# A four-stage kernel on one core: routing ranks made batch by batch, and the tail of the scan moved

## The chip, the cores and the metric

The kernel runs on one core of a Trainium2 chip. The metric is the device time of one execution in microseconds (us). A core has TensorE (PE, with its weight loads PEld), VectorE (DVE), ScalarE (ACT), GpSimd (POOL) and SyncE (SP), which issues most transfers.

## The reference, cut to what matters

Layer 0 is a state-space block over 4 images of 32 x 32 places and 256 channels: a layer norm, a projection to 512, a 3 x 3 depthwise convolution, GELU, a selective scan with 64 states, a second layer norm, a projection back and a residual. Layer 1 is an attention without softmax, then 16 experts of which each token takes two:

```python
xs = ...                                  # scan of 1024 places, 512 channels, 64 states
x = src + (_layernorm(ys + x * D_skip, ln2_g, ln2_b) @ w_out + b_out)
t = to_tokens(x)
qkv = _ln_t(t) @ W_qkv + b_qkv            # q, k: centred by rows
kv = einsum('bnc,bnd->bcd', k2, v)        # k2, q2: squares, normalised
t = t + (v + einsum('bnc,bcd->bnd', q2, kv) / sqrt(N)) @ W_out + b_out
probs = softmax(_ln_t(t) @ gate_w + gate_b); top 2 of 16, weights renormalised
t = t + sum over the two: weight * ((silu(x @ w1) * (x @ w2)) @ w3)
```

## The kernel before, in words

There are 4096 tokens, in 4 batches of 8 tiles of 128 tokens. All work is in fp32 but for a few routing masks in bf16.

**The scan (to about 2802 us).** It goes over 8 units, each half a batch (512 places). In a unit, 64 states times 4 channel blocks make 256 slots. In each slot ScalarE makes a scaled input `bx` (L687) and a decay `da` (L695), PE turns `bx` (L701), VectorE runs the scan `h` (L712); every fourth slot GpSimd multiplies `h` by C (L719), and PE adds the result to a sum `y` in PSUM (L733). This part's order is written out by hand: `beside(u)` hands out lists of pieces of other work (the next units' convolution, `conv`; their step sizes, `dt_bc`; the last unit's layer norm and output, `after`), and each piece goes into a slot where its engine has room. All pieces share one PSUM bank, `bg`. At a unit's end `close_sum` copies `y` to `ysb` (L750).

**The tail (about 2802 to 2842 us).** Nothing stands beside the last half's output: `run(after_stats(u))`, the roots and `run(*after(u, None))` come one after another (L604 to L627), and write to the tensor `td` in memory. Then the weights of attention are loaded (`wqkv`, `wout` and their biases), centred and multiplied together (L949 to L1004: `wcat`, `wvT`, `bvo`, `bcat`), and `t_all` is loaded from `td` (L941).

**Attention (about 2842 to 3088 us).** Outside the hand-written parts a scheduler orders the instructions of each engine by its own costs. A batch makes statistics (L1011), `xh`, its transpose, then for each of 8 tiles `pqk` (L1037), `qk` (L1042), its square `sq` (L1045), `sums` (L1046), `pv` (L1054); then `q2T`, `k2`, `ksq`, `pkv` (L1089), `po` (L1134), the normed tokens `xe`, stored in `xd` (L1150), and the gate: `pgT`, `pg`, and two masks `hots` of each token's experts (L1193). PSUM holds three buffers for `pqk` and `pv` and two for the tag `po`. Much of a batch's gate work stands among the next batch's projections.

**The ordering (about 3088 to 3140 us).** Over all 32 tiles at once: the masks are added (`hot2`, L1220), counted over partitions by two products (`ptot`, `prank`), summed along tiles (`run`, L1230), turned into each expert's number of 128-row blocks and first block (`over`, `nb`, `end`, `first`), each block's expert (`done`, `ef`, `eid`), each pair's slot (`pick`, `sf`), and from it the one-hot masks `qh` (place in block, L1287) and `ih` (block, L1291). Products `pgp` (L1302) of these give each block's rows, `src` and `dst`.

**The experts (about 3140 to 3570 us).** A hand-written order goes over 74 blocks. SyncE reads `eid`, fetches three weights of 512 KB (L1340, L1353; six buffers, four blocks ahead); GpSimd gathers the rows `xb` (L1346) and scatters the result `yb` (L1397). The weights' pool `wp` is opened after the ordering's pools are closed, and the blocks of memory of closed pools are given out again.

**The end (to about 3603 us)** loads both results of each token and adds them (L1439).

## Time and profile before

| | us |
|---|---|
| median of 3 runs | 3609.48 |
| lowest, highest | 3608.98, 3614.11 |
| profiled execution, its time | 3609.15 |
| profiled execution, span from first to last instruction | 3607.3 |

| engine | busy us | share of the span |
|---|---|---|
| PE | 3245.6 | 90% |
| PEld | 2626.9 | 73% |
| DVE | 2981.9 | 83% |
| ACT | 2863.8 | 79% |
| POOL | 2484.2 | 69% |

The shares are means over stages with different limits, so they are read stage by stage: busy time in chosen windows says which engine fills a stage, the chain of waits says what follows on what where no engine does, and the lists by line give the length of one instruction of each kind. Line numbers are those of the kernel before.

### The profile page before, as it was taken

How to read it: one execution, taken by the hardware profiler on the slowest of the kernel's cores; microseconds unless marked ns; L12 is line 12 of the kernel's file. 1: busy time of each engine (PE TensorE's matmuls, PEld its weight loads, DVE VectorE, ACT ScalarE, POOL GpSimd, SP SyncE). 2: the span in 40 equal slices, each digit the busy share in tenths (PEclk: the TensorE clock that was granted, in tenths of full speed). 3: DMA queues.
4: the chain of work that ended last, by engine and by line, in shares of the span. 5: the costliest groups of instructions: out<-in, count | busy, mean ns of one | idle time of the engine just before them, and what ended most of it. 6: DMA issues, size and time to landing. Idle time of an engine off the chain costs nothing.

```text
span 3607.3 us, 60573 instructions
## 1 busy us (share of the span) xinstructions
PE 3245.6 (90%) x22292; PEld 2626.9 (73%) x22292; DVE 2981.9 (83%) x3398; ACT 2863.8 (79%) x4748; POOL 2484.2 (69%) x906
## 2 busy tenths in 40 slices
PE   8989999999998998999999989898999788599995
PEld 3678777777777777777777777777777455399985
DVE  5799999999999999999999999999999666622224
ACT  1799999999999999999999999999999244121211
POOL 0489878987897798879878987998888110033331
PEclk9999999999999999999999999999999999699997
DMA  3223222212222122222222122222121200299996
GB/s 101 64 55 76 56 64 65 61 57 58 71 69 60 62 62 61 64 63 66 60 64 64 57 59 54 55 58 57 55 60 55 73 24 12 100 381 325 319 302 236
DMA packets 355165, 334.41 MB, mean 93 GB/s; under 512 B 162081, under 2 KB 241441, under 8 KB 354866
## 3 DMA queue, kind: packets, MB, share of 16 engines
q1 hardware_dynamic: 334834, 306.21, 29.1%
q0 software_dynamic: 7104, 19.41, 1.6%
q10 hardware_dynamic: 12928, 4.89, 0.5%
q8 instruction: 177, 2.90, 0.3%
q14 instruction: 122, 1.00, 0.1%
HBM read 304.21 MB, written 25.69 MB: 91 GB/s over the span
## 4 chain that ended last, share of the span: by engine, by line
ACT 60%; PE 20%; DMA 8%; DVE 7%; issue 2%; POOL 0%; POOLq 0%; DVEq 0%; ACTq 0%; SPq 0%
ACT da L695 28%; ACT bx L687 28%; DMA yd<-yb,dst 6%; PE ps L701 4%; PE y L733 3%; PE p L1377 3%; DVE h L712 3%; PE pqk L1037 2%; PE bg L382 1%; PE pf L1389 1%; DMA xb<-xd,src 1%; PE pv L1054 1%; PE ps L382 1%; PE ps_t L120 1%; ACT L695 1%
## 5 line engine op out<-in xcount | busy, mean ns | idle before, releaser
L719 POOL TENSOR_TENSOR h<-h,cb_n 128x2048 f32<-128x2048 f32 x512 | 2143.6, 4192 | 416.7 <-DVE h L712 328.0
L701 PE MATMUL ps<-ident,bx 128*128 128x128 f32 x8192 | 1323.3, 283 | 197.8 <-DVE h L712 138.0
L687 ACT ACTIVATE bx<-dtxT,bT 128x512 f32<-128x512 f32 x2048 | 1451.5, 709 | 16.5 <-DVE dtxT L534 16.5
L695 ACT ACTIVATE da<-dt,l_conv_a_log_sb 128x512 f32<-128x512 f32 x2048 | 1452.2, 709 | 13.6 <-DVE h L712 13.3
L701 PEld LDWEIGHTS ps<-ident,bx 128*128 128x128 f32 x8192 | 937.2, 142 | 632.8 <-DVE h L712 307.9
L712 DVE TENSOR_TENSOR_SCAN h<-da,last,ps 128x512 f32<-128x512 f32 x1024 | 1231.6, 1263 | 30.3 <-ACT da L695 21.6
L733 PE MATMUL y<-ident,h 128*128 128x128 f32 x8192 | 1246.1, 275 | 5.7 <-POOL h L719 5.6
L712 DVE TENSOR_TENSOR_SCAN h<-da,ps 128x512 f32<-128x512 f32 x1024 | 1189.5, 1207 | 49.4 <-ACT da L695 32.6
L733 PEld LDWEIGHTS y<-ident,h 128*128 128x128 f32 x8192 | 974.5, 143 | 7.8 <-POOL h L719 6.7
L1383 DVE TENSOR_TENSOR hT<-s,p 128x256 f32<-128x256 f32 x148 | 62.4, 421 | 336.4 <-ACT s L1382 336.4
L1377 PE MATMUL p<-xT,w 128*128 128x128 f32 x2368 | 291.6, 277 | 0.5 <-ACT xT L1366 0.5
L1377 PEld LDWEIGHTS p<-xT,w 128*128 128x128 f32 x2368 | 285.1, 194 | 4.8 <-ACT xT L1366 0.9
L1382 ACT ACTIVATE s<-p 128x256 f32<-128x256 f32 x148 | 56.9, 384 | 275.5 <-PE p L1377 275.5
L1397 POOL DMA_INDIRECT yd<-yb,dst x74 | 73.2, 990 | 264.5 <-DMA yd<-yb,dst 185.9
L382 PE MATMUL bg<-pad,dgc 128*128 128x512 f32 x432 | 222.2, 596 | 0.0
L1346 POOL DMA_INDIRECT xb<-xd,src x74 | 72.1, 975 | 132.8 <-DVE dst L1318 108.7
L1389 PE MATMUL pf<-w,hT 128*128 128x256 f32 x592 | 153.3, 382 | 0.1
L1051 POOL TENSOR_TENSOR t_all<-t_all,bcat 128x256 f32<-128x256 f32 x32 | 23.0, 747 | 164.6 <-ACT xh L1023 159.9
L1389 PEld LDWEIGHTS pf<-w,hT 128*128 128x128 f32 x592 | 101.7, 192 | 8.2 <-DVE hT L1383 0.5
L1366 ACT COPY xT<-px 128x256 f32<-128x256 f32 x74 | 27.6, 372 | 77.5 <-PE px L1364 77.5
L382 PEld LDWEIGHTS bg<-pad,dgc 128*128 128x128 f32 x432 | 65.5, 192 | 0.0
L382 PE MATMUL ps<-pad,dgc 128*128 128x512 f32 x144 | 64.0, 605 | 0.7 <-DVE e L487 0.7
(287 smaller groups left out, 2056.5 us busy)
## 6 DMA issues: line engine op xcount, KB each, us to landing
cb_n<-cd SPq DMA_DIRECT2D x512, 256.0 KB, 3.3
w<-in_L_ffn_w_dram SPq DMA_DIRECT2D x222, 512.0 KB, 6.2
dgc<-diags SPq DMA_DIRECT2D x84, 192.0 KB, 3.1
y<-yd SPq DMA_DIRECT2D x8, 1024.0 KB, 9.6
last<-h SPq DMA_DIRECT2D x256, 2.0 KB, 2.9
xr<-in_x_dram SPq DMA_DIRECT2D x32, 128.0 KB, 3.2
td<-xr SPq DMA_DIRECT2D x32, 128.0 KB, 3.3
t_all<-td SPq DMA_DIRECT2D x4, 1024.0 KB, 10.0
```

The lines of the kernel that those rows point to most:

```text
L382: nc.tensor.matmul(made["bg"].rearrange("p (h w) -> p h w", w=WW), made["dgc", m * 3 + i][:, j, :], pads[m][:, half * ROWS + i : (half + 1 ...
L687: nc.scalar.activation(t, made["dtxT", u][:, j, :], AF.Copy, scale=made["bT", u][:, j, n : n + 1])
L695: nc.scalar.activation(t, made["dt", u][:, m, :], AF.Exp, scale=A[:, m, n : n + 1])
L701: nc.tensor.transpose(t[:, blk(j, P)], made["bx", s, j][:, blk(m, P)], ident)
L712: nc.vector.tensor_tensor_scan(h[:, m, 1:], made.pop(("da", s, m)), made.pop(("dbx", s, m)), 0.0 if seg == 0 else last[b][:, n, m : m + 1] ...
L719: nc.gpsimd.tensor_tensor(h[:, :, :BANK], h[:, :, 1:], over_middle(made["c", s], DK), ALU.mult)
L733: nc.tensor.matmul(made["y", u][j][:, blk(m, P)], made["h", s][:, m, blk(j, P)], ident, is_transpose=True, start=n == 0 and m == 0, stop=n ...
L1037: nc.tensor.matmul(pqk.rearrange("p s c -> p (s c)"), xhT[:, ck, blk(i, P)], wcat[:, ck, : 2 * C], start=(ck == 0), stop=(ck == CK - 1),)
L1346: nc.gpsimd.indirect_dma_start(t, None, xd[:, :], bass.IndirectOffsetOnAxis(src[:, i : i + 1], 0))
L1377: nc.tensor.matmul(p12[:, j, s, :], on[w, i][:, ck, blk(h + j, P)], on["xT", i][:, ck, :], start=(ck == 0), stop=(ck == CK - 1),)
L1389: nc.tensor.matmul(on["pf", i], on["hT", i][:, hk, :], on["w3", i][:, hk, :], start=(hk == 0), stop=(hk == HK - 1),)
L1397: nc.gpsimd.indirect_dma_start(yd[:, :], bass.IndirectOffsetOnAxis(dst[:, i : i + 1], 0), yb, None)
```

## The change

**Attention's weights.** A new list of pieces, `matrices()`, loads, centres and multiplies attention's weights. `beside(6)` hands it out among the slots 20 to 245 of unit 6. Its tiles take the place of the padded images `pads`, in a pool `keep0` that stays open. The weights stay in three tensors (`wqk`, `wvo`, `brow`) in place of `wcat` and `bcat`.

**The last half's output.** The run of `after_stats`, roots and `after` behind the scan is gone. `ysb`, `w_o` and `b_o` live in `keep0`. `t_all` is loaded from `td`, its last half from the input `x`. `last_half()` stands ahead of batch 1 of attention in the program and adds the output into `t_all` there; the norm's root comes from `Sqrt` and a reciprocal, as in attention.

**Ranks and rows.** Each batch of attention now makes `hot2`, its counts (`pc`), ranks (`run`), slots and the masks `qh` itself, with a running count per expert handed from batch to batch. A pair's slot is counted within its expert, and the expert's first block is added only to the block number (`bh`). After the last batch come the counts of blocks, `first`, `bh`, `eid` (from one column over partitions, turned by PE, in place of a table of 79 x 16), `ih` and the products.

**The weights' memory.** `wp` is opened ahead of the ordering's pools.

In PSUM, `ps_w` is opened ahead of `ps_y`. `junk` and `fold` have one buffer in place of two.

```diff
+    keep0 = ctx.enter_context(tc.tile_pool(name="keep0", bufs=1))
+    w_o = keep0.tile([P, DK, C], F32, name="l0_conv_w_out_sb")
+    b_o = keep0.tile([P, C], F32, name="l0_conv_b_out_row")
...
+        ps_w = l0.enter_context(tc.tile_pool(name="ps_w", bufs=3, space=PSUM))
         ps_y = l0.enter_context(tc.tile_pool(name="ps_y", bufs=1, space=PSUM))
-        ps_w = l0.enter_context(tc.tile_pool(name="ps_w", bufs=3, space=PSUM))
...
-            pad = w0.tile([P, HH + 2, WW + 2], F32, name=f"pad{m}")
+            pad = keep0.tile([P, HH + 2, WW + 2], F32, name=f"pad{m}")
...
+        def matrices():
+            wqk = keep0.tile([P, CK, 2 * C], F32, name="wqk", tag="pad0")
+            wvs = keep0.tile([P, 2, CK, C], F32, name="wvs", tag="pad1")
+            brow = keep0.tile([P, 4 * C], F32, name="brow", tag="pad2")
+            bqk, bvo, bout = brow[:, : 2 * C], brow[:, 2 * C : 3 * C], brow[:, 3 * C :]
+            made["mats"] = wqk, wvo, bqk, bvo, bout
+            rough = keep0.tile([P, 2 * BANK + P], F32, name="rough", tag="pad3")
...
+            def load():
+                nc.sync.dma_start(out=wqk, in_=w_in[:, :, : 2 * C])
+                nc.sync.dma_start(out=wv, in_=w_in[:, :, 2 * C :])
+                nc.sync.dma_start(
+                    out=wout, in_=a["L1_attn_W_out"].rearrange("(k p) n -> p k n", p=P)
+                )
+                nc.sync.dma_start(out=bqk, in_=b_in[: 2 * C].partition_broadcast(P))
+                nc.sync.dma_start(out=bout, in_=a["L1_attn_b_out"].partition_broadcast(P))
+                with nc.allow_non_contiguous_dma(reason="small, once"):
+                    nc.sync.dma_start(out=bv, in_=b_in[2 * C :].rearrange("(k p) -> p k", p=P))
...
+            def sums(w, n, ck):
+                if ck == 0:
+                    take()
+                nc.tensor.matmul(
+                    made["bg"][:, :n], ones1, w[:, ck, :], start=(ck == 0), stop=(ck == CK - 1)
+                )
+            def off_columns(w, n, ck):
+                nc.vector.scalar_tensor_tensor(
+                    w[:, ck, :], made["bg"][:, :n], -1.0 / C, w[:, ck, :], ALU.mult, ALU.add
+                )
+            def rows_of(w, m):
+                nc.vector.tensor_reduce(m, w.rearrange("p (s c) -> p s c", s=2), AX.X, ALU.add)
+            def off_rows(w, m, s):
+                nc.vector.scalar_tensor_tensor(
+                    w[:, blk(s, C)], m[:, s : s + 1].to_broadcast([P, C]), -1.0 / C,
+                    w[:, blk(s, C)], ALU.mult, ALU.add,
...
+            todo = [
+                piece(1, "SP", 0, load),
+                piece(1, "DVE", 0.2, lambda: nc.vector.memset(ones1, 1.0)),
+            ]
+            for w, n in ((wqk, 2 * C), (wv, C)):
+                for ck in range(CK):
+                    todo.append(piece(
+                        8 if ck == 0 else 1, "PE", 0.88 * n / BANK,
+                        lambda w=w, n=n, ck=ck: sums(w, n, ck), "" if ck else "take",
+                    ))
+                for ck in range(CK):
+                    todo.append(piece(
+                        1 if ck else 3, "DVE", 0.69,
+                        lambda w=w, n=n, ck=ck: off_columns(w, n, ck), "free" if ck else "",
+                    ))
+            for w, m in ((wqk[:, 0, :], mean[:, 0, :]), (wqk[:, 1, :], mean[:, 1, :]), (bqk, bmean)):
+                todo.append(piece(1, "DVE", 0.69, lambda w=w, m=m: rows_of(w, m)))
+                for s in range(2):
+                    todo.append(piece(1, "DVE", 0.42, lambda w=w, m=m, s=s: off_rows(w, m, s)))
+            for m in range(CK):
+                todo.append(piece(
+                    1, "PE", 0.22, lambda m=m: turn_wv(m), "" if m else "take"
+                ))
+            todo.append(piece(3, "DVE", 0.69, lambda: put(wvT), "free"))
+            for ck in range(CK):
+                todo.append(piece(
+                    1, "PE", 0.88, lambda ck=ck: mult_wv(ck), "" if ck else "take"
+                ))
+            todo.append(piece(3, "DVE", 0.69, lambda: put(wvo), "free"))
+            todo.append(piece(
+                1, "DVE", 0.3, lambda: nc.vector.tensor_copy(bvw, over_last(bv, P))
+            ))
+            todo.append(piece(2, "PE", 0.88, lambda: mult_bv(), "take"))
+            todo.append(piece(
+                3, "DVE", 0.42, lambda: nc.vector.tensor_copy(bvo, made["bg"][:, :C]), "free"
+            ))
+            todo.append(piece(
+                2, "POOL", 0.73, lambda: nc.gpsimd.tensor_tensor(bout, bvo, bout, ALU.add)
+            ))
...
+            return todo
...
-            t = acts.tile([P, TPB, DN], F32, name="ysb", bufs=1)
+            t = keep0.tile([P, TPB, DN], F32, name="ysb")
...
+            if v == n:
+                lists.append([(matrices(), MATS)])
...
+        MATS = (20, 245)
...
-        alone = True
-        u = len(units) - 1
-        run(after_stats(u))
-        logs(made["rs"], made["mv"][:, :, 1])
-        roots_after(u)
-        run(*after(u, None))
...
+    counts = [l1.tile([P, NE], F32, name=f"counts{b}") for b in range(NB)]
+    within = l1.tile([P, 2, NTA], F32, name="within")
+    qh = l1.tile([P, 2, NTA, BS], BF16, name="qh")
...
+        tbs = [t_all[:, b * NT : (b + 1) * NT, :] for b in range(NB)]
+        for b in range(NB - 1):
+            nc.sync.dma_start(out=tbs[b], in_=rows(td, b))
+        nc.sync.dma_start(out=tbs[-1][:, :TPB, :], in_=rows(td, NB - 1)[:, :TPB, :])
+        nc.sync.dma_start(out=tbs[-1][:, TPB:, :], in_=rows(xf, NB - 1)[:, TPB:, :])
...
+        wqk, wvo, bqk, bvo, bout = made["mats"]
...
+        def last_half():
+            ysb = made["ysb", len(units) - 1]
+            _, rs = statistics(ysb, "ln1", TPB)
+            for j in range(TPB):
+                t = tbs[-1][:, TPB + j, :]
+                nc.gpsimd.tensor_tensor(t, t, b_o, ALU.add)
+                ps = ps_b.tile([P, BANK], F32, name="ps_l", tag="po")
+                for m in range(DK):
+                    nc.tensor.transpose(ps[:, blk(m, P)], ysb[:, j, blk(m, P)], ident)
+                yT = sm.tile([P, BANK], F32, name="yT")
+                nc.vector.tensor_copy(yT, ps)
+                po = ps_b.tile([P, C], F32, name="po_l", tag="po")
+                for m in range(DK):
+                    nc.tensor.matmul(
+                        po, yT[:, blk(m, P)], w_o[:, m, :], start=(m == 0), stop=(m == DK - 1)
+                    )
+                nc.vector.scalar_tensor_tensor(
+                    t, po, rs[:, j : j + 1], t, ALU.mult, ALU.add
+                )
         for b in range(NB):
+            if b == 1:
+                last_half()
             tb = tbs[b]
             _, rs = statistics(tb, "ln2")
...
+            hot2 = sm.tile([P, NE, NT], F32, name="hot2")
+            nc.vector.tensor_tensor(
+                hot2, hot[0].rearrange("p g e -> p e g"), hot[1].rearrange("p g e -> p e g"), ALU.add
+            )
+            flat = hot2.rearrange("p e g -> p (e g)")
+            pc = ps_b.tile([P, 2, NE * NT], F32, name="pc", tag="po")
+            nc.tensor.matmul(pc[:, 0, :], every, flat, start=True, stop=True)
+            nc.tensor.matmul(pc[:, 1, :], before, flat, start=True, stop=True)
+            run = sm.tile([P, NE, NT], F32, name="run")
+            rflat = run.rearrange("p e g -> p (e g)")
+            nc.vector.tensor_tensor_scan(
+                rflat, keep.rearrange("p e g -> p (e g)"), pc[:, 0, :], 0.0, ALU.mult, ALU.add
+            )
+            if b == 0:
+                nc.vector.tensor_copy(counts[b], run[:, :, NT - 1])
+            else:
+                nc.vector.tensor_tensor(counts[b], run[:, :, NT - 1], counts[b - 1], ALU.add)
+            nc.vector.tensor_tensor(rflat, rflat, pc[:, 0, :], ALU.subtract)
+            nc.vector.tensor_tensor(rflat, rflat, pc[:, 1, :], ALU.add)
+            if b > 0:
+                nc.vector.tensor_tensor(run, run, over_last(counts[b - 1], NT), ALU.add)
+            sf = sm.tile([P, 2, NT], F32, name="sf")
+            for k in range(2):
+                pick = sm.tile([P, NT, NE], F32, name="pick")
+                nc.vector.tensor_tensor(pick, hot[k], run.rearrange("p e g -> p g e"), ALU.mult)
+                nc.vector.tensor_reduce(sf[:, k, :], pick, AX.X, ALU.add)
+            slot = sm.tile([P, 2, NT], I32, name="slot")
+            nc.vector.tensor_copy(slot, sf)
+            nc.vector.tensor_single_scalar(slot, slot, BS.bit_length() - 1, ALU.arith_shift_right)
+            gs = slice(b * NT, (b + 1) * NT)
+            nc.vector.tensor_copy(within[:, :, gs], slot)
+            qb = sm.tile([P, 2, NT], BF16, name="qb")
+            nc.vector.scalar_tensor_tensor(
+                qb, within[:, :, gs], -float(BS), sf, ALU.mult, ALU.add
+            )
+            for k in range(2):
+                nc.vector.tensor_tensor(
+                    qh[:, k, gs, :], over_middle(places, NT), over_last(qb[:, k, :], BS),
+                    ALU.is_equal,
+                )
...
+    wp = ctx.enter_context(tc.tile_pool(name="wp", bufs=6))
...
+        nbi = rt.tile([P, NE], I32, name="nbi")
+        nc.vector.tensor_scalar(nbi, counts[-1], float(BS - 1), None, ALU.add)
+        nc.vector.tensor_single_scalar(nbi, nbi, BS.bit_length() - 1, ALU.arith_shift_right)
...
+        pick = rt.tile([P, 2 * NTA, NE], F32, name="pick")
         nc.vector.tensor_tensor(
+            pick, hot_all.rearrange("p k g e -> p (k g) e"), over_middle(first, 2 * NTA), ALU.mult
         )
+        bf = rt.tile([P, 2, NTA], F32, name="bf")
+        nc.vector.tensor_reduce(bf.rearrange("p k g -> p (k g)"), pick, AX.X, ALU.add)
+        bh = rt.tile([P, 2, NTA], BF16, name="bh")
+        nc.vector.tensor_tensor(bh, bf, within, ALU.add)
+        done = rt.tile([P, NE], F32, name="done")
+        nc.vector.tensor_scalar(done, end, block_p, None, ALU.is_le)
+        ef = rt.tile([P, 1], F32, name="ef")
         nc.vector.tensor_reduce(ef, done, AX.X, ALU.add)
+        pe = ps_r.tile([1, P], F32, name="pe")
+        nc.tensor.transpose(pe, ef, ident)
+        nc.vector.tensor_scalar(eid, pe[:, :NBLK], float(NE - 1), None, ALU.min)
...
-                qh = rt2.tile([P, GC, BS], BF16, name="qh", bufs=2)
-                nc.vector.tensor_tensor(
-                    qh, over_middle(places, GC), over_last(qb[:, k, gs], BS), ALU.is_equal
-                )
...
-                        pgp.rearrange("p s n -> p (s n)"), qh[:, j, :],
+                        pgp.rearrange("p s n -> p (s n)"), qh[:, k, c * GC + j, :],
```

## The prediction

> **What bounds the kernel now.** I read the page's 40 slices first: ScalarE is above 90% busy to about 2800 us (the scan), TensorE from about 3140 us to 3560 us (the experts), and neither in between. So I cut the run by stage with busy time by window; the columns after the length are PE, PEld, DVE, ACT, POOL, then the granted clock, the DMA share and GB/s.
>
> ```profile
> 2140.00:2473.00 333.00, 303.53 (x2209) 244.33 (x2210) 319.80 (x295) 330.90 (x534) 295.50 (x91) 0.98 0.23 56
> 2800.00:2842.00 42.00, 23.26 (x88) 16.39 (x88) 22.77 (x71) 7.55 (x14) 5.42 (x18) 0.86 0.51 157
> 2907.00:2929.00 22.00, 22.00 (x78) 13.41 (x78) 18.75 (x48) 8.80 (x24) 0.00 (x0) 1.00 0.00 1
> 3095.00:3140.00 45.00, 12.90 (x68) 9.08 (x68) 33.06 (x41) 5.41 (x4) 5.01 (x5) 0.50 0.12 36
> 3200.00:3300.00 100.00, 100.00 (x764) 95.41 (x764) 23.17 (x55) 20.91 (x55) 33.38 (x34) 1.00 1.00 345
> ```
>
> Unit 6 of the scan (row 1) is ScalarE-bound. The tail between scan and attention (row 2) fills no engine: it is a chain. The projections of attention's batch 1 (row 3; batches 2 and 3 look the same) are TensorE-bound, with VectorE 3.2 us short of full. The ordering (row 4) is VectorE. The experts (row 5) are TensorE.
>
> The chain of waits shows both gaps (start, duration, engine, tile, line). First the tail:
>
> ```profile
> 2800.87 1.65 PE y L733 x13
> 2802.55 1.29 DVE ysb L750 x2
> ...
> 2820.02 5.24 DMA l_attn_b_qkv_row<-in_L_attn_b_qkv_dram
> ...
> 2826.98 3.51 PE pw L953 x4
> ...
> 2841.56 0.52 ACT xh L1023
> ...
> 2842.12 3.94 PE ps_t L120 x12
> ```
>
> The scan's last sum closes at 2802.5 and attention's first transpose starts at 2842.1. Between stand the last half's output one piece after another, then the load of attention's weights, then their centring and products (L953 to L1004), then batch 0's statistics. Now the ordering:
>
> ```profile
> 3095.09 2.06 PE ptot L1225 x2
> ...
> 3109.27 1.47 DVE ih L1291
> 3110.75 2.20 DVE qh L1287
> ...
> 3129.31 2.30 PE pgp L1302 x16
> ...
> 3133.73 6.28 DMA xb<-xd,src
> ```
>
> It runs from the last choice of experts (about 3093.8) over `dst` (3133.0) and the first gather to the first expert transpose at 3140.1. On SyncE's own queue the first expert weight waits for it:
>
> ```profile
> SPq L1340 <- DVE dst L1318: 26.0, 1, 26.0
> ```
>
> The memory of the weights lies over the ordering's tiles, so they start at 3133.2, though `eid` is ready at 3105.8.
>
> **What the Trainium skill says.** "VectorE: DVE Perf Modes", section on the fixed extra latency: it gives an fp32 two-input operation (N+151)/0.96 ns, so small operations pay mostly a constant. The trace agrees: 512 elements take 688 ns (L1042), 128 take 284 ns (L1173). I size absent shapes by it. "DMA: Bandwidth & Descriptors", Issuing engines are not separate DMA queues: transfers from SyncE and GpSimd interleave on the same 16 engines. The trace agrees: gathers take 3.1 us at best and 5.3 us in the median while weights stream. "TensorE: Matmul & The Clock Gate", the HAM clock gate: an idle array falls to half clock. The rows above agree, with 0.50 in the ordering.
>
> **The change, part by part.** The places come from the changed kernel's instruction order, with its waits; the durations from the trace before.
>
> *1. Attention's weight work into unit 6.* SyncE issues 6 loads at slot 20. They wait for the pads, last read by the convolution in unit 5, so nothing on that queue is held; `cb_n` is fetched three steps (15 us) ahead. PE gets 5.6 us (two 512-column products at 0.86, eight of 256 columns at 0.43, four transposes at 0.11), GpSimd one 0.73 us add; both have 29 us and more free in this unit. VectorE gets 18 operations: 4 of 512 at 0.69, 3 reductions at 0.68, 8 of 256 at about 0.37, a copy of 0.42, two small of 0.2 and 0.3: 8.7 us, some 7.3 us net of the overlap of neighbours. Row 1 leaves it 13 us. That cover is thin: ScalarE's `da` has six buffers, and a late scan stalls it. I take +1.5 us, between 0 and +9.
>
> *2. The tail goes.* After it `ysb` is still copied out by 2803.9. The `t_all` load now waits only for the last scan step (ends 2796.5). The first of these loads took 7.8 us (four together: 7.8 to 11.8), so it lands at about 2804.4. In VectorE's order the 8 statistics of batch 0 have 4 of `ysb` (0.6 us net) and two of batch 1 mixed in: 10 x 0.33 + 4 x 0.6 + 13 x 0.11 = 7.1 us, then 0.6 to the root, reciprocal and first `xh`, and 0.5 for that. The first transpose starts at about 2812.7, against 2842.1: **-29.4 us**, from -32 (all in shadow) to -24 (loads at 11.8 us, the order less kind). Late next are these statistics. The GpSimd constants behind the last `h` cost about 1.3 us and end before `ysb` is needed.
>
> *3. The last half's output returns inside batch 1.* PE gets 16 transposes at 0.11 and 16 products with `w_o` at 0.43: 8.6 us, in a section where PE has none free, plus the two small `pc` products, 0.44. VectorE gets 4 x (0.69 + 0.48) = 4.7 us. Following both queues, with the three `pq` and two `po` buffers, from the fifth `pqk` on, PE ends 9.5 us later. GpSimd's four extra adds (0.74) lie in its 160 us of idle time. **+10 us**, from +8 to +15.
>
> *4. Ranks and rows by batch.* Each batch adds on VectorE `hot2`, `run`, three adds, two `pick` and two `sf` at about 0.3 (a scan 0.42), five small of 0.16 and two `qh` of 1024 at 1.17 (half of L1287's 2.28): 5.8 us, 4.9 net. Those of batches 0 to 2 stand in the next batch's projections, ahead of some `qk`. Behind a late `qk` queues its square on ScalarE and then the PSUM buffer that PE needs. VectorE has 3.2 us free there, so about 1.9 us shows: batches 2 and 3 give **+3.8 us**, from +1 to +10; batch 1's is within part 3. PE meets `pc` after the fifth `pqk`, just when `hot2` comes.
>
> *5. What stays of the ordering.* From the last choice of experts, by the new order: `hot2` 0.3, `pc` at half clock 0.9, small operations to 4.8, a `pick` over 1024 (1.2) and its reduction (1.2) with `qb` between to 7.4, two `qh` 2.2, `bh` and `eid` to 9.9, four `ih` and four `both` at 1.4 to 21.1, the last two groups of `pgp` to 24.3, seven small to 25.6 us. Before it was 3133.0 - 3093.8 = 39.2. **-13.5 us**, from -16 to -10.
>
> *6. Weights opened early.* They start at about 12 us of these 25.6 instead of at the end. PE never waited for them at 3140, so nothing is gained directly. Six blocks of 1.5 MB at 380 GB/s last about 24 us, so the first gather still meets them: 0, from -3 (a gather at the 3.1 us minimum) to +1 (7.3, the slowest). The experts and the end are untouched: 0.
>
> Sum: 1.5 - 29.4 + 10 + 3.8 - 13.5 = -27.6. Against the profiled execution, 3609.15 us, that is 3581.6; the median of the runs is 0.33 higher, so **3582 us**.
>
> **The rivals.**
> - *VectorE becomes the bound (13%).* Nothing hides its new work: +9 in unit 6, +14 in batch 1, +10 in batches 2 and 3. For it: 96% and 85% busy already, in-order. Against it: the new pieces are spread over 225 slots, and each batch has 5 us of VectorE idle before L1099. 1.5 becomes 9, 10 becomes 14, 3.8 becomes 10: 3599 us.
> - *More is won (12%).* The ordering work hides fully, the gather is at its minimum, unit 6 pays nothing and part 3 is at its low end: 1.5 + 3.8 + 3 + 2 us below the forecast, 3572 us. For it: the idle stretch before L1099 in each batch. Against it: `qh` stands before the last `qk`, not in that stretch.
> - *The experts slow (4%).* The rest before them shrinks by some 40 us, and if the granted clock fell below 1.00 there, 409 us of TensorE-bound work would stretch. At 0.94 the gain is gone; at 0.92 the cost is 36 us and the kernel is at 3618, slower. Against it: after 330 us of scan at 0.98 the clock was not cut.
> - *The change does not do what it says (3%).* If `t_all`, laid over the scan's memory, came only after other readers, part 2 shrinks to about half: 3597 us.
>
> **How the numbers follow.** The likeliest case has 68%. Its own bounds, not all at one end, give 3574 to 3592. Taking in most of the two larger rivals gives 3571 to 3598. A measurement here can tell 0.2% (7.2 us) from no change. The cases below 3602 make faster 0.92; same 0.05 (the first rival's far end, a clock near 0.94); slower 0.03.
>
> **What would show it.** Right: attention's first transpose about 10 us after the last `y`; batch 1 about 71 us long instead of 61, batches 2 and 3 about 63; `ih` within 10 us of the last choice; weights on SyncE ahead of `pgp`; the scan's end within 2 us of before. Wrong: a scan that ends over 5 us later, PE waiting for `qk` or `hot2` through the projections, a first `ln_st` waiting for `t_all`, or an experts stage that is not 430 us long.

## The result, and the profile after

The changed kernel takes 3599.85 us (median of 11 runs, 3594.91 to 3608.89), the kernel before, run beside it, 3612.66 us (11 runs): a ratio of 0.9959, 95% interval 0.9948 to 0.9970: 12.8 us faster by the medians, about 15 by the ratio. A second set of runs gave 0.9973 (0.9963 to 0.9983). The forecast of 3582 us, with 3571 to 3598 as its range, asked for about twice the gain, 27.6 us. The two profiled executions differ by 11.1 us (spans 3607.3 and 3596.2 us).

The stages of the kernel after, by window; columns as before (length, PE, PEld, DVE, ACT, POOL, granted clock, DMA share, GB/s). The rows are unit 6, the gap between scan and attention, batch 1's projections, the ordering, and a piece of the experts:

```profile
2146.00:2479.00 333.00, 298.03 (x2193) 247.61 (x2193) 322.88 (x307) 328.06 (x527) 290.84 (x91) 0.97 0.25 60
2811.00:2823.00 12.00, 2.12 (x17) 1.88 (x17) 9.33 (x37) 3.67 (x7) 1.64 (x11) 0.75 0.97 312
2894.00:2926.00 32.00, 30.36 (x127) 20.38 (x125) 29.52 (x83) 11.79 (x30) 0.00 (x0) 1.00 0.00 1
3096.00:3127.00 31.00, 8.13 (x69) 6.94 (x69) 21.27 (x46) 5.29 (x4) 4.64 (x5) 0.61 0.62 211
3200.00:3300.00 100.00, 99.13 (x755) 94.31 (x754) 22.39 (x54) 20.31 (x54) 33.15 (x34) 1.00 0.99 329
```

In unit 6 ScalarE, the stage's bound, fell from 330.9 to 328.1 us of 333, and VectorE rose from 319.8 to 322.9: the scan is slower here, though no engine's share says why. The gap of 42 us has become 12. Batch 1's projections, now with the last half among them, leave PE 1.6 us and VectorE 2.5 of 32.

The new gap in order of time (start, duration, engine, line; in brackets the idle time before and its releaser):

```profile
2812.26 1.04 PE L861 MATMUL y<-ident,h 128*128 128x128 f32 x8
...
2813.01 1.29 DVE L878 COPY ysb<-y 128x512 f32<-128x512 f32 x2 [0.88 <-PE y L861]
...
2815.61 0.75 DVE L1078 BATCH_NORM_STATS2 ln_st<-t_all 128x6 f32<-128x256 f32 x2 [1.31 <-issue]
...
2816.36 0.66 DVE L1078 BATCH_NORM_STATS2 ln_st<-ysb 128x6 f32<-128x512 f32 x1
...
2822.85 1.27 PE L120 MATMUL ps_t<-ident,xh 128*128 128x128 f32 x3 [9.55 <-ACT xh L1113]
```

The scan's last product ends at 2813.30 and the first transpose starts 9.55 us later, behind statistics among which those of `ysb` stand, as the forecast had it. On SyncE's queue the first expert weight now waits for the expert number, and is issued at 3107.75, ahead of the products `pgp` (3110.57):

```profile
SPq L1435 <- DVE eid L1379: 23.7, 1, 23.7
```

Stage by stage, from the two profiled executions:

| stage | before | after | difference | forecast |
|---|---|---|---|---|
| start to the first copy of `ysb` (after unit 0) | 471.6 | 476.0 | +4.4 | none |
| from there to the last copy of `ysb` (its start) | 2330.9 | 2337.0 | +6.1 | +1.5 |
| from there to attention's first transpose | 39.6 | 9.8 | -29.7 | -29.4 |
| first transpose to `pkv` of batch 0 | 29.4 | 30.8 | +1.4 | 0 |
| batch 1, `pkv` to `pkv` | 60.9 | 72.0 | +11.1 | +10 |
| batches 2 and 3 | 122.4 | 127.8 | +5.4 | +3.8 |
| `pkv` of batch 3 to the last `pg` | 32.9 | 36.8 | +3.9 | 0 |
| last choice of experts to `dst` | 39.1 | 23.9 | -15.3 | -13.5 |
| `dst` to the first expert transpose | 7.2 | 7.2 | 0 | 0 |
| first three expert blocks | 9.9 | 11.4 | +1.5 | 0 |
| from there to the end | 457.3 | 457.5 | +0.2 | 0 |

The differences add up to the measured -11.1 within rounding; the 6.1 us from the last `pg` to the last choice are the same in both and left out. Both large gains are what was forecast or better. The loss lies in the plus signs: some 34 us in place of 15.3.

### The profile page after: what moved, and what is told of

It is laid out like the page before. It is cut to its first block, busy times and chain, and to the rows that moved or that the text cites. A ratio compares the mean times of both kernels' runs of the same rounds, so it can differ in the third digit from the quotient of the medians.

```text
span 3596.2 us, 60612 instructions
## 1 busy us (share of the span) xinstructions
PE 3242.0 (90%) x22305; PEld 2633.8 (73%) x22305; DVE 2982.2 (83%) x3449; ACT 2864.4 (80%) x4741; POOL 2482.7 (69%) x901
## 5 line engine op out<-in xcount | busy, mean ns | idle before, releaser
L815 ACT ACTIVATE bx<-dtxT,bT 128x512 f32<-128x512 f32 x2048 | 1472.1, 719 | 17.6 <-DVE dtxT L540 16.5
L823 ACT ACTIVATE da<-dt,l_conv_a_log_sb 128x512 f32<-128x512 f32 x2048 | 1473.3, 720 | 14.3 <-DVE h L840 13.3
L1141 POOL TENSOR_TENSOR t_all<-t_all,brow 128x256 f32<-128x256 f32 x32 | 23.1, 744 | 183.3 <-ACT xh L1113 183.3
L1135 ACT ACTIVATE sq<-qk 128x512 f32<-128x512 f32 x32 | 20.2, 630 | 60.6 <-DVE qk L1132 60.6
```

What stands on the lines that cost most here:

```text
L815: nc.scalar.activation(t, made["dtxT", u][:, j, :], AF.Copy, scale=made["bT", u][:, j, n : n + 1])
L823: nc.scalar.activation(t, made["dt", u][:, m, :], AF.Exp, scale=A[:, m, n : n + 1])
```

## The experiments

The first theory is that part 1 was priced too low, because six small operations of `matrices()` stand still while GpSimd works. In unit 6 the line `off_rows` (L699) has operations of 256 elements that should take about 0.4 us. All instructions of the line, with shortest, median and longest duration in ns:

```profile
L699 DVE SCALAR_TENSOR_TENSOR wqk<-w_mean,wqk x4: 1877/2505/4024, 2301.3 to 2343.6; 128x256 f32<-128x256 f32 x4
L699 DVE SCALAR_TENSOR_TENSOR brow<-b_mean,brow x2: 398/642/885, 2366.5 to 2375.7; 128x256 f32<-128x256 f32 x2
```

Here is the slowest of them, with GpSimd, VectorE and ScalarE (kernel after):

```profile
2343.17 4.18 POOL L847 TENSOR_TENSOR h<-h,cb_n 128x2048 f32<-128x2048 f32 x1
...
2343.61 4.02 DVE L699 SCALAR_TENSOR_TENSOR wqk<-w_mean,wqk 128x256 f32<-128x256 f32 x1
...
2348.80 0.73 ACT L823 ACTIVATE da<-dt,l_conv_a_log_sb 128x512 f32<-128x512 f32 x1 [0.59 <-DVE h L840]
...
2352.99 1.22 DVE L840 TENSOR_TENSOR_SCAN h<-da,ps 128x512 f32<-128x512 f32 x1 [0.90 <-PE ps L829]
```

GpSimd's product holds from 2343.17 to 2347.35; the VectorE operation, begun 0.44 us later, ends at 2347.63, 0.28 us after it. The other three slow ones end 0.28 us after a GpSimd product too. Behind it the scan is late: ScalarE waits 0.59 us for a buffer of `da`, and the scan then 0.90 us for PE. The Trainium skill states the cause, in "SBUF — State Buffer", section Who interferes with whom: an operation of VectorE with two inputs in SBUF (where all tiles lie that are not in PSUM) reads the second through the interface that GpSimd reads by; the shared interface is locked exclusively, and the order of issue decides who is blocked. The trace agrees: the scan `h` (1.15 to 1.28 us in all its calls) and L691 (0.67 us), each with an input in PSUM, keep their length beside such products. The rival was that VectorE has no room for 8.7 us in unit 6, whatever the operands.

**Other operands (e_psum).**

```diff
 def off_rows(w, m, s):
     nc.vector.scalar_tensor_tensor(
-        w[:, blk(s, C)], m[:, s : s + 1].to_broadcast([P, C]), -1.0 / C,
+        w[:, blk(s, C)], made["bg"][:, :C], -1.0 / C,
         w[:, blk(s, C)], ALU.mult, ALU.add,
     )
```

The bank `bg` is given free only after the last of the six.

> The six operations that take the row means off Wq, Wk and their bias in unit 6 read the PSUM bank in place of the broadcast mean, as first operand; number, size and engine stay (the values are not the right ones). Theory A, these operations stand still while GpSimd multiplies h, because both their operands lie in SBUF: the six fall from about 2.5 us (four) and 0.6 us (two) to 0.37 each, and the last ysb copy comes 4 to 7 us earlier after the first one than in the changed kernel (2337.0 us there, 2331 before). Theory B, VectorE has no room for 8.7 us in unit 6: their durations may fall, but the distance stays at 2336 to 2338 us.

The line's list in this kernel:

```profile
L699 DVE SCALAR_TENSOR_TENSOR wqk<-bg,wqk x4: 395/395/396, 2258.6 to 2264.7; 128x256 f32<-128x256 f32 x4
L699 DVE SCALAR_TENSOR_TENSOR brow<-bg,brow x2: 395/395/395, 2267.8 to 2269.2; 128x256 f32<-128x256 f32 x2
```

And ScalarE's timeline a little later:

```profile
2274.45 1.06 ACT L499 ACTIVATE e<-e 128x1024 f32<-128x1024 f32 x1 [1.70 <-DVE e L493]
```

All six take 0.395 us, three of them (2263.2, 2267.8 and 2269.2) wholly inside a GpSimd product: two operands in SBUF are the cause of the long durations. But the time did not come back: unit 6 took 333.2 us (before 328.2, after 332.6), and the kernel 3599.83 us (0.9962, 0.9949 to 0.9976). Held to one bank, the pieces stood in neighbouring slots; VectorE needed 1.44 us a slot where ScalarE gives 1.23, fell behind, and ScalarE waited 1.70 us for its `e`. The edit moved the pieces as well as their operands, so this run alone does not price the stalls. It shows that each theory can hold for a part: VectorE's sum over a unit does not decide, but whether it catches up where the piece stands.

**Off VectorE (e_pool).**

```diff
     nc.vector.tensor_reduce(m, w.rearrange("p (s c) -> p s c", s=2), AX.X, ALU.add)
+    nc.gpsimd.tensor_scalar(m, m, 1.0 / C, None, ALU.mult)
...
-    nc.vector.scalar_tensor_tensor(... -1.0 / C, ..., ALU.mult, ALU.add)
+    nc.gpsimd.tensor_tensor(w[:, blk(s, C)], w[:, blk(s, C)], m..., ALU.subtract)
...
-    nc.vector.tensor_copy(bvw, over_last(bv, P))
+    nc.gpsimd.tensor_copy(bvw, over_last(bv, P))
```

> The same six operations and the copy bvw go to GpSimd, and the mean is scaled there; the result is the same. Theory A (standing still beside GpSimd): the distance from the first to the last ysb copy falls from 2337 to about 2331 to 2332 us, and the kernel gains 5 us on the changed one, some 3595 us. Theory B (VectorE overfull): only 2 us of VectorE work are gone, so 2335 us. A third outcome, GpSimd too late with h: 2340 us or more.

Measured: 3594.58 us (5 runs; 0.9949, 0.9932 to 0.9967), unit 6 330.4 us. The distance of the two copies, 2335.8 us, is nearer to theory B; unit 7 was 1.1 us longer than in the kernel after, so unit 6 by itself tells more. Following ScalarE's `da` through unit 6 against the kernel before places the loss. In the kernel after it comes in two steps: about 1.2 us at the 50th to 60th us (beyond the 0.4 us that a second execution of the kernel before also shows there), and 2.1 us at the 170th to 190th, behind the last two of the four stalls (after the first two VectorE caught up). In e_pool the second step is gone and the first is unchanged. Of the +4.4 us, 0.4 is thus seen without any change, and 0.7 belongs to neither step and stays open. The first is here, in VectorE's timeline of the kernel after:

```profile
2220.76 0.67 DVE L691 SCALAR_TENSOR_TENSOR wqk<-bg,wqk 128x512 f32<-128x512 f32 x1
2221.34 1.21 DVE L840 TENSOR_TENSOR_SCAN h<-da,ps 128x512 f32<-128x512 f32 x1
2222.46 0.67 DVE L691 SCALAR_TENSOR_TENSOR wqk<-bg,wqk 128x512 f32<-128x512 f32 x1
2223.05 3.43 DVE L840 TENSOR_TENSOR_SCAN h<-da,ps 128x512 f32<-128x512 f32 x3
```

VectorE is idle for 0.2 us in all from 2209 to 2232 us, and was so in the kernel before at the same place: the two operations show nearly in full.

**A tie (e_lastmid, e_lastmid2, e_after).** The profile of e_lastmid, an experiment on attention told below, had a unit 6 of 341.7 us. GpSimd and VectorE in the timelines, of the kernel after:

```profile
2366.44 4.47 POOL L847 TENSOR_TENSOR h<-h,cb_n 128x2048 f32<-128x2048 f32 x1
2366.47 0.40 DVE L699 SCALAR_TENSOR_TENSOR brow<-b_mean,brow 128x256 f32<-128x256 f32 x1
```

and of e_lastmid, with ScalarE:

```profile
2367.42 4.17 POOL L847 TENSOR_TENSOR h<-h,cb_n 128x2048 f32<-128x2048 f32 x1
2367.44 4.43 DVE L699 SCALAR_TENSOR_TENSOR brow<-b_mean,brow 128x256 f32<-128x256 f32 x1
...
2373.04 0.72 ACT L823 ACTIVATE da<-dt,l_conv_a_log_sb 128x512 f32<-128x512 f32 x1 [3.44 <-DVE h L840]
```

Both begin within 0.03 us of each other. In the first VectorE goes through and GpSimd's product takes 4.47 us in place of 4.18; in the second GpSimd goes through, VectorE stands 4 us, and ScalarE 3.44. Being late, the second operation on `brow` then takes 4.10 us too; together they cost 9 us.

> The changed kernel once more, timed beside the two below. In two of six profiled executions with this unit 6 the two operations on the bias row (L699, brow) took 4.1 and 4.4 us in place of 0.4 and 0.9, and unit 6 ran 341.7 in place of 332.6 us. Theory A: a tie with GpSimd's product h, decided by chance in each execution; so single times of this kernel fall into two groups some 9 us apart (3594 to 3600 and 3603 to 3609 in the eleven seen), and this profile shows either 332.6 or 341.7 us for unit 6, nothing between. Theory B: it belongs to the kernels in which it was seen; then this one always shows 332.6.

e_after (the changed kernel once more): 3600.46 us (10 runs); unit 6 332.8 us.

> e_lastmid once more. Its unit 6 took 341.7 us, with two operations on the bias row (L699, brow) of 4.1 and 4.4 us; five profiles of kernels with the same unit 6 show 332.6 to 332.8 and 0.4 and 0.9. Theory A, a tie decided by chance in each execution: this profile shows 332.6 with the larger chance (about 5 in 7). Theory B, something of this kernel decides it: 341.7 again. The three batches from the first pkv to the last take 192 to 193 us again in either case.

e_lastmid2 (e_lastmid once more): unit 6 332.8 us, bias rows 0.40 and 0.88 us, the three batches 193.6 us, a little over the expectation. The same kernel shows both, so chance decides. Of eight profiles with this unit 6 two lost the tie. The recorded starts don't tell which: GpSimd's is the earlier one in all eight, by 0.006 to 0.028 us, and by 0.018 and 0.023 in the two lost, so the skill's order of issue can't be read from them to that precision. The single times of e_after (3592 to 3609 us) don't fall into two clear groups as expected, since other parts scatter as much.

**The start, and the PSUM pools (c_before, e_psswap).**

> The kernel before once more, one profiled execution. The question is the 4.4 us by which the changed kernel reached the first copy of ysb later (476.0 against 471.6 us), before anything that the change moves has run. Theory A, chance: the start differs from one execution to the next, so this one comes out anywhere from 470 to 477 us, and the distance from the first to the last ysb copy stays within 1 us of 2331 us. Theory B, the order of the PSUM pools or the place of the padded images costs 4 us: this one shows 471.6 us within 0.5.

c_before: first copy at 475.5 us, 2332.4 us to the last, 1.4 more than in the first profile, where at most 1 was expected. In fourteen profiles the first copy comes at 471.6 to 478.8 us, whatever the kernel: the +4.4 is chance.

```diff
-        ps_w = l0.enter_context(tc.tile_pool(name="ps_w", bufs=3, space=PSUM))
         ps_y = l0.enter_context(tc.tile_pool(name="ps_y", bufs=1, space=PSUM))
+        ps_w = l0.enter_context(tc.tile_pool(name="ps_w", bufs=3, space=PSUM))
```

> The two PSUM pools of the scan are opened in the old order, one profiled execution. In units 1 to 5 the changed kernel loses 1.6 us in all against the one before, by the same amounts in each execution (337.0 for 336.3 us in unit 2). Theory A, the place of the PSUM banks: the distances return to 340.3, 336.3, 340.3, 336.6 us. Theory B, it comes from elsewhere (w_o, b_o and the padded images in another pool): they stay at 340.5, 337.0, 340.5, 336.7. The first copy of ysb comes anywhere from 470 to 477 us in both.

e_psswap: 340.5, 337.0, 340.5, 336.7 us for units 1 to 4, as in the kernel after; 3599.72 us. The order of the pools is not what costs 1.5 us in units 1 to 5. What does stays open.

**The last half's output (e_nolast, e_lastmid).** e_nolast leaves out the call of `last_half()`.

> The last half's output is left out of attention (its tokens keep only the residual input). Theory A, batch 1 is TensorE-bound and the added products show in full: from pkv of batch 0 to pkv of batch 1 it takes 62 to 63 us in place of 72.0 (10 us less, the size that the prediction gave this part), batches 2 and 3 stay at 63.2 and 64.6. Theory B, the ranks of batch 0 and their wait for hots are what lengthens batch 1 and the last half fills gaps: 66 us or more. The kernel ends 5 to 10 us earlier than the changed one.

e_nolast: batch 1 took 62.5 us in place of 72.0, batches 2 and 3 64.5 and 65.0; 3582.35 us (0.9919, 0.9898 to 0.9941). The last half costs batch 1 9.5 us, by theory A; over the three batches it is 7.8 us, since batches 2 and 3 were 1.3 and 0.4 us longer here. The median lies 17.5 us under the changed kernel's, where 5 to 10 were expected; the rest is in stretches that scatter by as much. e_lastmid moves it:

```diff
-    if b == 1:
-        last_half()
...
     nc.vector.tensor_copy(kvT, pkv)
+    if 0 < b < NB - 1:
+        last_half((2 * b - 2, 2 * b - 1))
```

> The last half's output stands behind the products pkv of batches 1 and 2 (two tiles each), where PE waits for sums and roots, and no longer ahead of batch 1. Theory A, its 9.5 us show because the projections leave PE no gap: in the new place the four waits of 1.5 us and the waits for xe take in part of it, batch 1 falls from 71 to 72 us to 66 to 68, batch 2 rises from 63.2 to 64.2 to 65 to 67, and the sum of both falls by 2 to 4 us. Theory B, VectorE is behind in those stretches too and what is added there lengthens the batch in full: sum unchanged within 1 us.

e_lastmid: batches 1 to 3 took 62.7, 65.0 and 64.9 us, 192.6 together, against 199.8 with the last half ahead of batch 1 and 192.1 without it. The move saves 7.3 us (6.3 in e_lastmid2), more than either theory said: the output costs only 0.5 to 1.5 us there. The median is 3591.46 us (0.9935, 0.9912 to 0.9957). Batches 2 and 3 of e_nolast by window (a row is `pkv` to `pkv`):

```profile
2913.25:2977.78 64.53, 55.79 (x212) 34.98 (x212) 46.41 (x124) 25.17 (x62) 5.80 (x8) 0.91 0.05 17
2977.78:3042.79 65.01, 56.79 (x212) 36.12 (x213) 46.54 (x124) 25.18 (x62) 5.73 (x8) 0.89 0.05 17
```

The same rows of e_lastmid, with two tiles of the last half in each:

```profile
2925.08:2990.09 65.01, 57.90 (x236) 37.74 (x236) 49.32 (x133) 25.19 (x62) 5.80 (x8) 0.95 0.05 17
2990.09:3055.03 64.94, 57.84 (x232) 37.52 (x233) 49.10 (x133) 25.49 (x63) 5.80 (x8) 0.94 0.05 17
```

By the prediction's prices PE has 4.3 us more products in each row (two tiles at four times 0.11 and 0.43), but is only 2.1 and 1.1 us busier, and its clock is 0.95 and 0.94 in place of 0.91 and 0.89. Put where PE used to wait for sums and roots, the products fill gaps, and the clock is higher: 0.94 to 0.95 in both batches of all four profiles with tiles there (e_lastmid, e_lastmid2, e_best, e_best2), 0.88 to 0.92 in the other ten.

**The clock at attention's end.** The products `pkv` of batch 3 in PE's timeline of the kernel after:

```profile
3053.48 10.01 PE L1179 MATMUL pkv<-k,xh 128*128 128x256 f32 x32 [0.55 <-ACT k L1157]
```

And in e_psum, whose attention is the same:

```profile
3054.18 3.95 PE L1182 MATMUL pkv<-k,xh 128*128 128x256 f32 x12 [0.27 <-ACT k L1160]
3058.41 4.58 PE L1182 MATMUL pkv<-k,xh 128*128 128x256 f32 x20 [0.28 <-ACT k L1160]
```

The same 32 products take 10.01 or, gap included, 8.81 us. From the start of `pkv` of batch 3 to that of the last group of `pg`, the twelve profiles of changed kernels show 33.6 to 33.8 us five times and 35.3 to 36.3 seven times; both profiles of the kernel before show 32.4. The granted clock goes with it: 0.87 to 0.90 in the five short ones, 0.78 to 0.86 in the seven long. Two executions of one program show both (e_lastmid, then e_lastmid2); the third row is the kernel before:

```profile
3055.03:3090.96 35.93, 31.20 (x108) 20.98 (x109) 18.01 (x50) 9.27 (x25) 0.00 (x0) 0.78 0.09 30
3048.65:3082.37 33.72, 28.29 (x109) 18.27 (x109) 17.56 (x50) 9.26 (x25) 0.00 (x0) 0.90 0.09 32
3054.92:3087.36 32.44, 27.75 (x108) 18.53 (x108) 17.60 (x50) 9.26 (x25) 0.00 (x0) 0.89 0.10 33
```

"TensorE: Matmul & The Clock Gate" of the Trainium skill, on the HAM clock gate, says that PE falls to half clock after an idle window of about 3.4 us and that these windows run on regardless of the work, which would make it a matter of phase. The two values for one program fit, and the stretches at half clock in the records last 3.4 us or multiples of it; that the phase is the reason was not tested. So some 2.5 of the +3.9 us is chance. The other 1.2 to 1.4 is in every profile of a changed kernel. In e_lastmid2 neither clock nor VectorE's busy time differs from before (0.90, 17.6 us), so its cause stays open.

**The masks `qh` (e_qhlate).**

```diff
-    for k in range(2):
-        nc.vector.tensor_tensor(qh[:, k, gs, :], ..., over_last(qb[:, k, :], BS), ALU.is_equal)
...  in the ordering, beside ih
+    nc.vector.tensor_tensor(qh[:, k, gs, :], ..., over_last(qb[:, k, gs], BS), ALU.is_equal)
```

> All masks qh are made in the ordering again (one of 2048 elements beside each ih), only qb is made by batch. Theory A, qh (2.2 us on VectorE in one piece ahead of some qk) is what lengthens batches 2 and 3: from pkv to pkv they take 61.5 to 62.5 us in place of 63.2 to 65, and the stretch from the last choice to dst grows from 23.4 us by the six masks of the earlier batches, 6.6 us, to 30. Theory B, the lengthening comes from the many small operations and from PE's two pc products: the batches stay over 63 us, and qh by batch is a gain of some 6 us. With A the total is within 2 us of the changed kernel, with B 4 to 7 us slower.

e_qhlate: 70.8, 64.2, 63.4 us for the batches, 25.6 us from the last `hot` to `dst` (23.4 on the same count in the kernel after), 3594.48 us (4 runs; 0.9941, 0.9924 to 0.9959). The edit is only half of what was meant: of the four larger masks the scheduler put the two for batches 0 and 1 into attention (2990.7 and 2998.1 us), so 2.2 us came to the ordering, not 6.6. The sum of the batches fell by 1.4 us against the kernel after. Theory A asked for more: `qh` is a small part of the lengthening. Theory B's total, 4 to 7 us slower, did not come: the median is 5 us lower, with intervals that overlap, and this although the profiled execution was the other one with a lost tie (unit 6 341.7 us). What `qh` does can be seen in PE's timeline of the kernel after, at the end of batch 2's projections:

```profile
2986.04 0.92 PE L120 MATMUL ps_t<-ident,sq 128*128 128x128 f32 x5 [1.27 <-ACT sq L1135]
```

PE stands 1.27 us for the square of a late `qk`, in batch 3 as in batch 2. Neither profile of the kernel before has this wait; in e_qhlate it is gone from batch 3, whose projections hold no `qh` there, and in e_best (below) from both.

**The weights' memory (e_wplate).**

```diff
-    wp = ctx.enter_context(tc.tile_pool(name="wp", bufs=6))
     with tc.tile_pool(name="rt", bufs=1) as rt, ...
...
+    wp = ctx.enter_context(tc.tile_pool(name="wp", bufs=6))
     with tc.tile_pool(name="ffn", bufs=2) as ffn, ...
```

> The weights' memory is opened behind the ordering again, the rest as in the changed kernel. By the prediction's step 6, nothing is gained by opening it early: the first expert transpose stays 7.2 us behind dst, within 1 us, the second to fourth blocks' transposes shift by less than 1 us, and the total stays within 2 us of the changed kernel. The rival: the weights that come 12 us earlier were what let the first blocks run on time; then the stretch from the first expert transpose to the end grows by 5 to 12 us.

e_wplate: the first expert transpose comes 8.4 us after `dst` (7.2 with the early weights), where a shift of at most 1 us was expected; the third block comes 0.6 us later. From `dst` to the end it took 483.1 us, but with early weights the same stretch took 468.2 to 482.9 in eleven profiles. This scatter follows PE's waits for the gathered rows `xb`, in the kernel after and in e_after, the same program:

```profile
PE px L1463 <- DMA xb<-xd,src: 10.1, 11, 2.3
PE px L1463 <- DMA xb<-xd,src: 3.5, 5, 1.4
```

The stretch took 476.0 and 469.5 us. Over all fourteen profiles, 3.5 to 7.4 us of such waits (from 3150 to 3550 us) go with 468.2 to 473.6, 8.5 to 10.6 with 474.3 to 478.4, and 12.6 to 13.8 with 481.5 to 483.1; what makes the gathers late was not tested. e_wplate has the longest waits, 13.8, but e_psswap with early weights has 13.2. The median is 3607.2 us (17 runs; 0.9977, 0.9964 to 0.9990), 7 us above the changed kernel's, with an interval that overlaps e_after's. Opening early is worth about 1 us; whether it is worth more stays open.

**What the experiments point to (e_best, e_best2).** e_best joins e_pool and e_lastmid, spreads the two subtractions of L691 over slots and calls the masks of a batch behind the next batch's `pkv`; e_best2 leaves the masks where they were.

```diff
-    1 if ck else 3, "DVE", 0.69, ... off_columns(w, n, ck)
+    4 if ck else 3, "DVE", 0.69, ... off_columns(w, n, ck)
...
     nc.vector.tensor_copy(kvT, pkv)
+    if b > 0:
+        masks()
```

> The row means and bvw on GpSimd, the second subtraction of column means four slots behind the first in place of one, one or two qh of a batch behind the next batch's projections, and the last half's output in two parts behind the products pkv of batches 1 and 2. By the stages seen so far: no operation of unit 6 stands still, so 330 us or less in each execution (and 329 if the step of 1.2 us at its 55th us came from the two subtractions in neighbouring slots), 2 to 4 us better than the changed kernel's better group and 11 better than the other; batches 1 to 3 together 192 to 193 us in place of 199.9. Sum 9 to 12 us below the changed kernel's better group (3597): 3585 to 3588 us. The rival, that what the last half gains comes back in the last batch or in the experts: 3592 us or more.

> As e_best, but with both qh of a batch where the changed kernel has them, ahead of the next batch's last qk. If qh ahead of qk costs PE its buffers, this one is 1 to 3 us slower than e_best over batches 1 to 3; if the small operations and pc are what remains, both agree within 1 us there.

e_best: 3582.73 us (6 runs; 0.9923, 0.9907 to 0.9938), 17.7 us below e_after, which ran beside it. Unit 6 took 329.9 us, 0.5 less than e_pool: of the step at the 55th us 0.4 went. The two subtractions, now four slots apart but in the same full stretch, still cost about 0.9 us: their neighbourhood was not the reason. The batches took 61.7, 64.9 and 64.9 us, 191.5 in place of 199.8 in the first profile of the changed kernel and 202.4 in e_after. The kernel came out 2 us under the expectation. e_best2: 3586.63 us (0.9927, 0.9912 to 0.9943), the batches 192.9 us. The masks behind `pkv` give 1.4 us there; over the whole kernel the two can't be told apart.

## Why the prediction was wrong

In the profiled pair 16.5 us of the forecast gain are missing. The largest share that belongs to the change is part 1 (4.6 us, of which 1.5 lies outside unit 6 and stays open), and the step that failed is its price: lengths taken without regard to operands and neighbours, set against VectorE's free time summed over a unit. Some 7 us are chance (the start, and the half clock at attention's end). The rest are smaller terms.

- **Part 2, right.** -29.4 forecast, -29.7 measured, with the statistics late next, mixed with those of `ysb`, as it said. The first statistic waited 1.3 us; it started 8.6 us after the first load of `t_all` was issued (2807.0), so it most likely waited for that load.
- **Part 5, right.** -13.5 forecast (its own figures, 25.6 less 39.2, give -13.6), -15.3 measured, inside its range.
- **Part 3, right in size and reason.** +10 forecast, +11.1 measured in batch 1, of which leaving it out takes away 9.5 (7.8 over the three batches). That it need not cost this was not seen: the prediction priced it where the change put it.
- **Part 6, right as far as is shown:** 0 forecast with -3 as one end; e_wplate shows about 1 us gained, and leaves open whether it is more.
- **Part 1, the term that failed most.** "8.7 us, some 7.3 us net" priced each operation alone (those of 256 elements at 0.37 us; the same operation, L967, took 0.42 in the kernel before, where GpSimd was idle), and let them hide in VectorE's 13 us over the unit. Measured: four of about 0.4 took 1.88 to 4.02 us, the copy `bvw` 1.21 in place of 0.30. In place of the forecast +1.5 unit 6 gave +4.4 us: about 2.1 for the stalls, about 1.2 for two operations where VectorE has no room, 0.4 chance, 0.7 open. Units 1 to 5 gave 1.5 us whose cause stays open. In two of eight profiles the lost tie adds 9 us; unit 6 is then 13.4 us longer than before, beyond the upper bound of +9, for a reason that the prediction did not have.
- **Part 4, right in kind, low in size.** +3.8 forecast for batches 2 and 3 (4.9 less 3.2 is 1.7 a batch, not 1.9, so +3.4 by its own figures), +5.4 measured, +7.2 in e_after. The wait that it named, for the square behind a late `qk`, is there, with 1.27 us a batch. The part of `qh` in batches 1 to 3 is about 1.5 us, seen in two pairs of profiles. PE was 1.5 and 2.2 us busier there, more than two `pc` products (0.44); its clock, 0.91 and 0.90 in place of 0.92, is no term of the sum. Nor were +1.4 in batch 0 (29.1 to 30.8 us in twelve profiles, so partly chance) and +3.9 at the end of batch 3, some 2.5 of it from the half clock.
- **The start** (+4.4) and the first expert blocks (+1.5; 9.9 to 11.5 us in all profiles) are scatter of single executions.

The rival whose time came out, 3599 us, was "VectorE becomes the bound". That is luck: it asked for +9 in unit 6, +14 in batch 1 and +10 in batches 2 and 3, where +4.4, +11.1 and +5.4 came, and the rest was made up by terms it did not have. Its reason held only in places: VectorE is not the bound of unit 6, but it was full at the 55th us, and it stood still for GpSimd. Of the signs named for wrong, one came in full: a scan that ends more than 5 us later (10.5, of them 4.4 chance). Two came small: PE's wait behind a late `qk` (1.27 us) and a first `ln_st` that waits, most likely for `t_all` (1.3 us).

## What to carry to other kernels

Price a moved operation by its operands and by what runs beside it in the new place, not by its length in the old one, and ask for room in that place, not over the stage. Work for an engine that waits often is cheapest inside those waits: over the three batches the same products cost 7.5 to 10.3 us ahead of a full stretch (six profiles against e_nolast) and 0.5 to 1.5 us within the gaps, where the clock was also higher. Stages compared over several profiles tell effects from chance where medians of few runs can't.

## What the runs showed of the hardware

- A VectorE operation of 0.4 us with both inputs in SBUF can take up to 4.43 us beside a GpSimd product of 4.2 us; the other way GpSimd loses 0.29 us. Where both start within 0.03 us, either can happen in one program, and 9 us of the kernel's time go with it; the recorded starts don't tell which.
- The same copy from SBUF to SBUF, `bvw`, shows 1.21 us in unit 6, where it ends 0.15 us after a GpSimd product, against 0.30 in the tail of the kernel before (L996).
- At attention's end a mean granted clock of 0.78 goes with 35.9 us, one of 0.90 with 33.7, in two executions of one program.
- In the same batches the clock was 0.94 to 0.95 with products in PE's gaps and 0.88 to 0.92 without them.
- The experts take 468 to 483 us in fourteen profiles, along with 3.5 to 13.8 us of PE's waits for gathered rows.
